# A two-layer image block on one core: layer 0's input normalisation moved from GpSimd to ScalarE, its loads and moments moved, and layer 1's first pass with the order of every engine written out

## The chip, the core and the metric

The kernel runs on one core of a Trainium2 chip. The core has a matrix engine (PE; its weight loads are shown as PEld), VectorE (DVE), ScalarE (ACT), GpSimd (POOL) and SyncE (SP), which here issues all DMA transfers. Each engine works through its own queue in order and waits on semaphores for the others. The metric is the time of one execution on the device in microseconds (us). Before the change it is 9212.45 us, the median of 3 runs (9209.08 to 9218.67).

## The reference

The input `x` has 4 images of 64 channels and 256 × 256 pixels, in f32. Two layers each add a branch to `x`, and each branch begins with a group norm over 32 groups of 2 channels (`_gn`):

```python
x = x + L0(gn(x));  x = x + L1(gn(x))

# L0: 64 -> 3*170 channels; a gate, a 3x3 depthwise branch and a spectral branch on 8x8 patches
gate, x_sp, x_fr = split(einsum('oi,bihw->bohw', w_in, x), 3)
sp = depthwise_conv3x3(x_sp, w_dw)
fr = irfft2(rfft2(patches8x8(x_fr)) * fft_weight)
out = einsum('oi,bihw->bohw', w_out, gelu(gate) * (sp + fr))

# L1: two state-space blocks, along rows (d = 0) and along columns (d = 1), then a 1x1 fusion
fx = layer_norm(x) * g + b                    # over the 64 channels of each pixel
h  = 2 * Re(C @ [scan forwards, scan backwards](B @ fx)) + D * fx
x  = gelu(h) + fx;  fx2 = layer_norm(x) * g2 + b2
y  = fx2 @ enc.T @ dec.T + fx2                # both directions, concatenated, then fusion_w
```

## The kernel before

**Layer 0.** An image is worked in 32 strips of 8 rows (`NS0`), 128 strips in all, in one software pipeline: while strip `cur` is in work, some steps of the next strip (`ahead(...)`) and of the strip before (`behind(...)`) are put between its own. The 128 partitions hold 64 channels twice, for even and odd rows or for two halves of a strip.

`load(b, s, nm, rs)` issues the DMA loads of one strip: `pr` (the patches, two transfers of 64 partitions), `at` (5 rows for each half, with the neighbours, two transfers) and `er` (4 rows for each half, two transfers). In the same call it normalises them with `normalise` (L156), a TENSOR_SCALAR on GpSimd that adds the negated mean and multiplies by the inverse deviation: `pn` from `pr` in two instructions, `at` in place, and `en` from `er`. `load` is called at the top of a strip's body, for the next strip. `at` has 3 buffers, `er` 3, `pr`, `pn` and `en` 2.

From `pn`, PE makes the spectral inputs (`spec1`, copied to SBUF as `hs` by ACT at L708; `spec2`, multiplied by the spectral weights into `hw` by VectorE). From `at`, VectorE makes sums and differences of neighbouring columns (`outer_in`, `middle_in`), which PE multiplies by the depthwise weights (`products`; ACT copies one half as `m3`, L769; VectorE joins the halves in `middle`). The last 42 hidden channels take another way: `inputs_b` makes them on PE, ACT copies them to `xat` (L743, and the row that two strips share at L734), and nine taps (`tap_b`) sum them up: tap 0 on ACT (L842), taps 1 to 8 on VectorE (L625). `gate_a` and `gate_b` make the gates on PE, with the Gelu on ACT (L804, L835). `fuse_*`, `project`, `residual` and `finish` end a strip, take its statistics for layer 1 and store it to `x1d`.

The moments of the next image are gathered meanwhile: `stat_load` brings one part of 32 a strip, `count` takes two BATCH_NORM_STATS instructions on it, and in the body of the last strip but one the last part is counted and `norm_of` makes mean and inverse deviation (an aggregate on VectorE, two small matmuls with VectorE work between, a power on GpSimd). The first strip of the next image needs them to be normalised.

**What sets the order.** The program is a list of instructions; a scheduler places each engine's instructions, by their dependencies, an estimate of their times and their place in the list. Calls through `mm` (PE) and through `vec` (VectorE, class `InOrder`) are kept in the order of the list by `tc.keep_in_program_order`. ACT, GpSimd and SP are left to the scheduler; in layer 1's first pass VectorE is as well.

**Layer 1.** For each image there are three stages: `pass_a` (first pass), `scan`, `pass_b` (second pass). `pass_a` works in 16 strips of 16 rows (`NS1`), in a pipeline in which strip `n` is centred while strip `n - 1` gets its deviation, strip `n - 2` is normalised and strip `n - 3` summarised. Its steps:

- `centre(g, i)`, for four parts: PE takes the channel mean off (`pc`), ACT writes `xc` and its square `sq` (L1059, L1060).
- `sums`, `rstd_of`, `widen`: PE sums the squares (`pv`), ACT copies the sums, PE transposes them, VectorE adds the epsilon (`ve`, L1076), GpSimd takes the power -1/2 (`rs`, L1077), and VectorE spreads it over 64 channels (`rw`, L1083, one buffer).
- `affine(g, i)`, for four parts: PE transposes `rw` (`pr`), VectorE multiplies (`z`, L1091), ACT applies gain and bias twice, for the two directions (`fv` L1095, `fh` L1099).
- `mirrored`: stores `fv` and `fh` to `fxd` and makes sums and differences of mirrored halves (`sd`, L1111): two instructions on VectorE for the columns, two on GpSimd for the rows.
- `summary_columns` and `summary_rows`: PE multiplies these by the state matrices (`pt`, `ps`), ACT copies one half (`m`, L1125, L1144), and VectorE places sum and difference in the state arrays (L1127, L1128; L1148, L1149).

Of the kernel before, what the change touches and what calls it, by code (L numbers as in the profile page):

```python
# [16 lines left out]
C = 64  # L17
HID = 170
S = 256
# [89 lines left out]
def tile_kernel(ctx: ExitStack, tc: tile.TileContext, x, cst, w0, winp, wdwp, w1, out):  # L109
# [45 lines left out]
    def normalise(o, i, nm, rs):  # L155
        nc.gpsimd.tensor_scalar(o, i, nm, rs, ALU.add, ALU.mult)  # L156
# [27 lines left out]
    with ExitStack() as l0:  # L184
# [83 lines left out]
        with ExitStack() as l1w:  # L268
# [347 lines left out]
            norm = group_norm(moments(new(gpool, [P, 2], "mv"), stats1), pw, "pw", "1")  # L616
# [4 lines left out]
        class InOrder:  # L621


            def __getattr__(self, name):
                return lambda *args, **kw: tc.keep_in_program_order(getattr(nc.vector, name)(*args, **kw))  # L625

        vec = InOrder()
# [11 lines left out]
        out_stats, last_at, n_loads = {}, {}, [0]  # L639

        def load(b, s, nm, rs):
            if s == 0:
                out_stats[b] = new(wk, [P, 2 * NS0, 6], "stats2")
            r0 = s * R0
            er = new(ld, [P, 4, S], "er", 3)
            pr = new(ld, [P, R0, 128], "pr")
            at, xat = ats[n_loads[0] % 3], xats[n_loads[0] % 2]
            n_loads[0] += 1
            for k in range(2):
                h = slice(k * C, (k + 1) * C)  # L650
                nc.sync.dma_start(out=pr[h], in_=x[b, :, r0 : r0 + R0, k * 128 : (k + 1) * 128])
# [7 lines left out]
            pn = new(wk, [P, 8, 2, R0, 8], "pn")  # L659
            for w in range(2):  # L660
                normalise(pn[:, :, w], pr[:, :, w * 64 : (w + 1) * 64].rearrange("p r (t c) -> p t r c", c=8), nm, rs)
            lo, hi = (1 if s == 0 else 0), (4 if s == NS0 - 1 else 5)
            normalise(at[:, lo:hi, 1 : S + 1], at[:, lo:hi, 1 : S + 1], nm, rs)
            if s == 0:
                nc.gpsimd.memset(at[0:C, 0, 1 : S + 1], 0.0)
                normalise(at[C:P, 0, 1 : S + 1], at[C:P, 0, 1 : S + 1], nm[C:P], rs[C:P])
            if s == NS0 - 1:
                nc.gpsimd.memset(at[C:P, 4, 1 : S + 1], 0.0)
                normalise(at[0:C, 4, 1 : S + 1], at[0:C, 4, 1 : S + 1], nm[0:C], rs[0:C])

            v14, v23 = new(wk, [P, 5, S], "v14"), new(wk, [P, 5, 2, 128], "v23")
            en = new(wk, [P, 4, S], "en")
            normalise(en, er, nm, rs)
            xen = new(wk, [P, 4, S + 2], "xen")
            return {
                "er": er, "at": at, "pn": pn, "en": en, "b": b, "s": s, "stats2": out_stats[b], "xat": xat, "xen": xen,
                "v14": v14.rearrange("p r (c k) -> p r k c", k=2), "v23": v23, "v": v14,
                "hs": new(wk, [P, 2, 4, 2, HID], "hs", 1), "hw": hws[s % 2],
            }
# [15 lines left out]
        def spec1(t, i):  # L695

            ps = new(pp, [P, 2, 512], "two")
            tiles = TILES[i]
            n = len(tiles)
            for k, tile_ in enumerate(tiles):  # L700
                for h in range(2):
                    p = slice(h * C, (h + 1) * C)
                    mm(
                        ps[:, h, k * HID : (k + 1) * HID], lhsT=t["pn"][p, tile_].rearrange("p w r c -> p (w r c)"),
                        rhs=wt0("wfr")[p, h * HID : (h + 1) * HID], start=True, stop=True,
                    )
            hs = t["hs"][:, tiles[0] % 2, tiles[0] // 2 : tiles[0] // 2 + 3] if n == 3 else t["hs"][:, :, 3]
            nc.scalar.copy(hs.rearrange("p k h c -> p h k c"), ps[:, :, : n * HID].rearrange("p h (k c) -> p h k c", k=n))  # L708
# [17 lines left out]
        def inputs_b(t):  # L726

            b, s = t["b"], t["s"]
            if s == 0:
                ps = new(pp, [P, 2, 512], "two").rearrange("p q (r c) -> p (q r) c", c=S)  # L730
                mm(ps[:, 0], lhsT=xb, rhs=t["at"][:, 0, 1 : S + 1], start=True, stop=True)
                nc.scalar.copy(t["xat"][:, 0, 1 : S + 1], ps[:, 0])
            else:
                nc.scalar.copy(t["xat"][:, 0], last_at[b][:, 4])  # L734
# [8 lines left out]
            nc.scalar.copy(t["xat"][:, 1:5, 1 : S + 1], ps)  # L743
            last_at[b] = t["xat"]
# [3 lines left out]
        def products(t, half, name, third):  # L748
# [20 lines left out]
            nc.scalar.copy(t["m3"], ps.rearrange("p e k m c -> p e k (m c)")[:, :, 1])  # L769
# [27 lines left out]
        def gate_a(t, half):  # L797
# [6 lines left out]
            nc.scalar.activation(t["ge"], pg.rearrange("p e x -> p (e x)"), AF.Gelu)  # L804
# [21 lines left out]
        def gate_b(t):  # L826
# [8 lines left out]
            nc.scalar.activation(t["geb"], ps, AF.Gelu)  # L835

        def tap_b(t, k):
            dy, dx = k // 3, k % 3
            src = (t["xat"][:, 0:4], t["xen"], t["xat"][:, 1:5])[dy]
            if k == 0:  # L840
                t["acc"] = new(wk, [P, 4, S], "acc")
                nc.scalar.activation(t["acc"], src[:, :, dx : dx + S], AF.Copy, scale=taps[:, 0:1])  # L842
# [43 lines left out]
        cur = load(0, 0, *norm)  # L886
# [11 lines left out]
        nxt_stats = None  # L898
        for b in range(nb):
            for s in range(NS0):  # L900
                if b + 1 < nb:
                    if s == 0:
                        nxt_stats = new(wk, [P, 2 * NS0, 6], "stats1")
                        counted = {0: stat_load(ld, b + 1, 0)}
                    if s + 1 < NS0:
                        counted[s + 1] = stat_load(ld, b + 1, s + 1)
                if s + 1 < NS0:
                    nxt = load(b, s + 1, *norm)
                elif b + 1 < nb:
                    nxt = load(b + 1, 0, *norm)  # L910
                else:
                    nxt = None

                def count(s, k):
                    if b + 1 < nb and s + 1 < NS0:
                        vec.bn_stats(nxt_stats[:, 2 * s + k, :], counted[s][:, k * 512 : (k + 1) * 512])
# [19 lines left out]
                count(s, 0)  # L936
                count(s, 1)
                behind(fuse_a, 1)
                products(cur, 0, "m23", False)
                middle(cur)  # L940
# [8 lines left out]
                behind(residual)  # L949
                behind(finish, 0)  # L950
# [23 lines left out]
                if s == NS0 - 2 and b + 1 < nb:  # L974
                    for k in range(2):
                        vec.bn_stats(nxt_stats[:, 2 * s + 2 + k, :], counted[s + 1][:, k * 512 : (k + 1) * 512])
                    norm = norm_of(nxt_stats)
# [58 lines left out]
    def pass_a(b, x0):  # L1036
        with ExitStack() as es:
# [17 lines left out]
            def centre(g, i):  # L1055
# [3 lines left out]
                nc.scalar.activation(xc, ps, AF.Identity, bias=off)  # L1059
                nc.scalar.activation(sq, ps, AF.Square, bias=off)  # L1060
                g["xc", i], g["sq", i] = xc, sq

            def sums(g):
# [5 lines left out]
                nc.scalar.copy(g["sums"], ps)  # L1069

            def rstd_of(g):
# [4 lines left out]
                nc.vector.tensor_scalar(ve, ps.rearrange("p (n c) -> p n c", c=32)[:, :, 0:2], LN_EPS, None, ALU.add)  # L1076
                nc.gpsimd.tensor_tensor(r, ve.rearrange("p n c -> p (n c)"), mhalf, ALU.pow)  # L1077
                g["rs"] = r

            def widen(g):  # L1080

                g["r"] = new(wk, [P, 32, C], "rw", 1)
                nc.vector.tensor_copy(g["r"], g.pop("rs").unsqueeze(2).to_broadcast([P, 32, C]))  # L1083

            def affine(g, i):
# [5 lines left out]
                nc.vector.tensor_tensor(  # L1091
# [3 lines left out]
                nc.scalar.activation(  # L1095
# [3 lines left out]
                nc.scalar.activation(  # L1099
# [4 lines left out]
            def mirrored(s, g):  # L1104

                for d, n, e in ((1, 4, nc.vector), (0, 8, nc.gpsimd)):
                    f = g.pop("fv" if d else "fh")
                    nc.sync.dma_start(out=fxd[b][s, d], in_=f.rearrange("p a b -> p (a b)"))
                    for k, op in enumerate((ALU.add, ALU.subtract)):
                        t = g["sd", d, k] = new(wk, [P, n, 1024 // n], f"sd{d}", 3)  # L1110
                        e.tensor_tensor(t, f[:, :n], f[:, : n - 1 : -1], op)  # L1111

            def summary_columns(g, s, k):
# [8 lines left out]
                if k == 0:  # L1122
                    return
                m = new(wk, [P, 256], "m")
                nc.scalar.copy(m, ps[:, 256:])  # L1125
                pv, mv = (t.rearrange("p (q g) -> p q g", q=16) for t in (ps[:, :256], m))
                nc.vector.tensor_tensor(along_columns(sf[1], 1, s), pv, mv, ALU.add)  # L1127
                nc.vector.tensor_tensor(along_columns(sb[1], 0, s), pv, mv, ALU.subtract)  # L1128

            def summary_rows(g, s, k):  # L1130
# [10 lines left out]
                if k == 0:  # L1141
                    return
                m = new(wk, [P, 2, P], "m")
                nc.scalar.copy(m, ps[:, :, P : 2 * P])  # L1144
                for hi in range(2):
                    c = slice(hi * C, (hi + 1) * C)
                    pv, mv = (t[:, :, c].rearrange("p k (r g) -> p k r g", r=4) for t in (ps, m))
                    nc.vector.tensor_tensor(along_rows(sf[0], 1, s, hi), pv, mv, ALU.add)  # L1148
                    nc.vector.tensor_tensor(along_rows(sb[0], 0, s, hi), pv, mv, ALU.subtract)  # L1149
# [9 lines left out]
            for n in range(NS1 + 3):  # L1159
                if n + 1 < NS1:  # L1160
                    got[n + 1] = {"x": load_strip(b, n + 1)}
                for i in range(4):
                    at(n, centre, i)
                    if i == 1:
                        at(n - 1, rstd_of)
                    at(n - 2, affine, i)
                    at(n - 3, (summary_columns, summary_rows)[i // 2], n - 3, i % 2)
                at(n, sums)
                if 0 <= n - 2 < NS1:
                    mirrored(n - 2, got[n - 2])  # L1170
                at(n - 1, widen)

# [63 lines left out]
    def pass_b(b):  # L1236

        with ExitStack() as es:
# [35 lines left out]

            class InOrder:


                def __getattr__(self, name):
# [282 lines left out]
```

## Time and profile before

The profiled execution took 9225.5 us, with a span of 9223.7 us from the first to the last instruction. Its stages, by the first and last instructions of each:

| stage | from (us) | to (us) | length (us) |
|---|---|---|---|
| preparation | 0 | 182 | 182 |
| layer 0, tap 0 of the first strip to tap 0 of the last | 182.0 | 4356.8 | 4174.8 |
| first pass of image 0, first centring to last placement | 4404.9 | 4680.5 | 275.7 |
| first pass of images 1, 2, 3 | 5601.2, 6805.7, 8011.1 | 5884.4, 7089.3, 8294.3 | 283.2, 283.6, 283.2 |
| second pass of image 0, first to last output | 4826.9 | 5601.1 | 774.2 |

A page shows one execution. An engine's busy share says how much of the span it worked, not whether its work was on the path. In a line of the time order the columns are: start, length, engine, source line, operation, output and inputs, shape, and how many instructions the line joins; a bracket at the end gives the engine's idle time just before it and what ended that. In a line of stages the columns are named in its first row; behind the engines come the granted PE clock, the share of the DMA engines and GB/s. A helper's line stands for all its calls: L197 is `mm` of layer 0, L625 is `vec` of layer 0, L1049 is `mm` of the first pass, L1273 and L1279 are `mm` and `vec` of the second.

### The profile page before, as it was taken

Reading aid. Unit: us, or ns where it says so; the run is one execution under the profiler, and the core shown is the slowest. Engines: PE = TensorE matmul, PEld = TensorE weight load, DVE = VectorE, ACT = ScalarE, POOL = GpSimd, SP = SyncE. Lnnn points to the kernel's source line nnn. Section 1 sums busy time; section 2 is a strip of 40 time slices with the busy share of each in tenths; the row PEclk is TensorE's granted clock in tenths of the full one; section 3 lists DMA queues with packets and bytes.
Section 4 is the critical chain, followed back from the end, with each engine's and each line's share of the span. In section 5 each row is a group of like instructions: output and inputs, shape, how many; then the busy total and the mean of one; then the engine's idle time right before and its main releaser. Section 6 shows DMA issues by size and latency. Waiting matters only on the chain. (4 is left out here: it accounts for less than half of the span.)

```text
span 9223.7 us, 183034 instructions
## 1 busy us (share of the span) xinstructions
PE 8686.5 (94%) x78454; PEld 5732.1 (62%) x78454; DVE 7299.4 (79%) x8833; ACT 2924.4 (32%) x4698; POOL 3345.0 (36%) x1798
## 2 busy tenths in 40 slices
PE   3999999999999999999889999999999999999999
PEld 2666666666666666666546665566665666665666
DVE  7999999998999989998677676767757667667776
ACT  2222222222222222222632225422245222362222
POOL 4222122221222212221664445644447444465443
PEclk9999999999999999999999999999999999999999
DMA  7444444444444433332622335323345233461332
GB/s 170 102 104 102 101 98 104 102 101 96 102 103 102 101 83 85 85 86 66 185 98 78 88 83 151 134 69 88 84 125 173 56 88 82 104 193 59 87 80 72
DMA packets 655578, 938.42 MB, mean 102 GB/s; under 512 B 43184, under 2 KB 584880, under 8 KB 619184
## 3 DMA queue, kind: packets, MB, share of 16 engines
q1 hardware_dynamic: 654768, 926.71, 38.6%
q8 instruction: 619, 10.14, 0.5%
q14 instruction: 191, 1.56, 0.1%
HBM read 583.86 MB, written 275.05 MB: 93 GB/s over the span
## 5 line engine op out<-in xcount | busy, mean ns | idle before, releaser
L197 PE MATMUL m<-v,sw 64*128 64x256 f32 (+1 forms) x8192 | 1546.0, 393 | 1.0 <-DVE v L625 0.9
L197 PEld LDWEIGHTS m<-v,sw 64*128 64x128 f32 (+1 forms) x8192 | 1136.7, 188 | 489.5 <-issue 350.4
L1376 POOL TENSOR_TENSOR xr<-xr,fx 128x512 f32<-128x512 f32 x512 | 651.3, 1272 | 1861.0 <-ACT xr L1375 1367.2
L1273 PE MATMUL pst<-fx,wb 64*128 64x256 f32 (+1 forms) x4992 | 1015.8, 437 | 37.4 <-DVE stm L1279 18.3
L625 DVE SCALAR_TENSOR_TENSOR acc<-xat,taps,acc 128x1024 f32<-128x1024 f32 x640 | 975.2, 1524 | 14.4 <-ACT acc L842 0.7
L156 POOL TENSOR_SCALAR pn<-pr,nm,rs 128x512 f32<-128x512 f32 x256 | 412.9, 1621 | 1376.9 <-issue 968.0
L804 ACT ACTIVATE ge<-two 128x1024 f32<-128x1024 f32 x256 | 262.8, 1027 | 1794.9 <-DVE hw L625 1706.4
L156 POOL TENSOR_SCALAR at<-at,nm,rs 128x1280 f32<-128x1280 f32 (+2 forms) x136 | 199.8, 1469 | 1624.9 <-DMA at<-in_x_dram 1565.5
L1273 PEld LDWEIGHTS pst<-fx,wb 64*128 64x128 f32 (+1 forms) x4992 | 508.1, 186 | 370.9 <-issue 244.3
L1406 POOL TENSOR_TENSOR rs<-ve,mhalf 128x32 f32<-128x32 f32 x128 | 695.5, 5433 | 99.3 <-DVE ve L1279 99.3
L1279 DVE SCALAR_TENSOR_TENSOR stm<-stm,step,pst 128x512 f32<-128x512 f32 x640 | 478.5, 748 | 232.8 <-PE pst L1273 219.3
L1377 ACT ACTIVATE sq<-xr 128x512 f32<-128x512 f32 x512 | 322.7, 630 | 875.4 <-POOL xr L1376 875.4
L197 PEld LDWEIGHTS m<-ct,hw 128*64 128x64 f32 x16384 | 509.3, 138 | 118.1 <-issue 118.1
L1273 PE MATMUL px<-wb,xr 128*128 128x128 f32 x4096 | 574.7, 284 | 0.0
L1279 DVE SCALAR_TENSOR_TENSOR sto<-sto,step,pst 128x512 f32<-128x512 f32 x512 | 382.8, 748 | 242.1 <-PE pst L1273 230.8
L625 DVE TENSOR_TENSOR hw<-two,wsp 128x1020 f32<-128x1020 f32 (+1 forms) x384 | 423.6, 1103 | 175.5 <-PE two L197 161.8
L1273 PEld LDWEIGHTS px<-wb,xr 128*128 128x128 f32 x4096 | 524.5, 194 | 54.2 <-issue 41.8
L1279 DVE TENSOR_TENSOR y<-px,rs 128x512 f32<-128x512 f32 x512 | 354.0, 691 | 231.4 <-PE px L1273 222.4
L1273 PE MATMUL ph<-sto,wb 128*64 128x128 f32 (+1 forms) x5120 | 528.0, 299 | 0.0
L197 PE MATMUL m<-ct,hw 128*64 128x64 f32 x16384 | 527.1, 223 | 0.0
L1273 PE MATMUL ph<-stm,wb 128*64 128x128 f32 (+1 forms) x5120 | 525.0, 299 | 0.0
L1273 PEld LDWEIGHTS ph<-stm,wb 128*64 128x64 f32 (+1 forms) x5120 | 408.9, 147 | 144.6 <-issue 128.1
(317 smaller groups left out, 16571.6 us busy)
## 6 DMA issues: line engine op xcount, KB each, us to landing
strip<-x1d SPq DMA_DIRECT2D x512, 256.0 KB, 7.3
fx<-fxd SPq DMA_DIRECT2D x128, 1024.0 KB, 6.9
at<-in_x_dram SPq DMA_DIRECT2D x248, 320.0 KB, 5.4
xen<-xat SPq DMA_DIRECT2D x256, 258.0 KB, 5.0
sx<-in_x_dram SPq DMA_DIRECT2D x256, 256.0 KB, 4.0
pr<-in_x_dram SPq DMA_DIRECT2D x256, 256.0 KB, 4.1
er<-in_x_dram SPq DMA_DIRECT2D x256, 256.0 KB, 4.5
x1d<-x SPq DMA_DIRECT2D x256, 256.0 KB, 3.6
```

Source lines behind the costliest of these rows:

```text
L156: nc.gpsimd.tensor_scalar(o, i, nm, rs, ALU.add, ALU.mult)
L197: tc.keep_in_program_order(nc.tensor.matmul(*args, **kw))
L625: return lambda *args, **kw: tc.keep_in_program_order(getattr(nc.vector, name)(*args, **kw))
L804: nc.scalar.activation(t["ge"], pg.rearrange("p e x -> p (e x)"), AF.Gelu)
L1273: tc.keep_in_program_order(nc.tensor.matmul(*args, **kw))
L1279: return lambda *args, **kw: tc.keep_in_program_order(getattr(nc.vector, name)(*args, **kw))
L1376: nc.gpsimd.tensor_tensor(xr, xr, fx, ALU.add)
L1377: nc.scalar.activation(sq, xr, AF.Square)
L1406: nc.gpsimd.tensor_tensor(r, ve.rearrange("p n c -> p (n c)"), mhalf, ALU.pow)
```

## The change

In layer 0, ACT normalises in place of GpSimd, by an activation with a scale and a shift (`scale_of` makes the shift from mean and deviation). `load` is taken apart: `load_patches` and `load_rows` issue the loads, and `normal_rows(n + 1)` and `normal_patches(n + 2)` normalise, both between `products(cur, 0, "m23", False)` and `middle(cur)`. The loads are issued behind `residual`: rows two strips ahead, patches three. The copy of the shared row of `xat` moves from `inputs_b` to `normal_rows`. The parts for the moments are loaded and counted two a strip in strips 0 and 1 and one a strip up to strip 29, at whose end `norm_of` now stands. ACT is kept in the order of the list (`act`).

In the first pass, ACT, VectorE and GpSimd are kept in the order of the list (`act`, `vec`, `gps`), steps are split (`scaled_in` from `affine`, `store` from `mirrored`, `place_columns` and `place_rows` from the summaries), and the body's order is written out. A strip is summarised four steps behind its centring, where it was three; the first half of the column summary stays at three.

```diff
-    def normalise(o, i, nm, rs):
-        nc.gpsimd.tensor_scalar(o, i, nm, rs, ALU.add, ALU.mult)
+    vec, act, gps = InOrder(nc.vector), InOrder(nc.scalar), InOrder(nc.gpsimd)
...
+        def normalise(o, i, b, p=slice(0, P)):
+            rs, shift = norm[b]
+            act.activation(o, i, AF.Identity, bias=shift[p], scale=rs[p])
+
+        def normal_patches(n):
...
+            pn = t["pn"] = new(wk, [P, 8, 2, R0, 8], "pn")
             for w in range(2):
-                normalise(pn[:, :, w], pr[:, :, w * 64 : (w + 1) * 64].rearrange("p r (t c) -> p t r c", c=8), nm, rs)
+                normalise(pn[:, :, w], pr[:, :, w * 64 : (w + 1) * 64].rearrange("p r (t c) -> p t r c", c=8), t["b"])
+
+        def normal_rows(n):
...
-            normalise(at[:, lo:hi, 1 : S + 1], at[:, lo:hi, 1 : S + 1], nm, rs)
+            normalise(at[:, lo:hi, 1 : S + 1], at[:, lo:hi, 1 : S + 1], b)
...
+            en = t["en"] = new(wk, [P, 4, S], "en")
+            normalise(en, t["er"], b)
...
+            if s > 0:
+                act.copy(t["xat"][:, 0], strips[n - 1]["xat"][:, 4])
...
+        parts = [(2 * s, 2 * s + 1) if s < 2 else (s + 2,) if s + 2 < NS0 else () for s in range(NS0)]
...
                 tap_b(cur, 2)
-                count(s, 0)
-                count(s, 1)
+                count()
                 behind(fuse_a, 1)
                 products(cur, 0, "m23", False)
+                if nxt is not None:
+                    normal_rows(n + 1)
+                normal_patches(n + 2)
                 middle(cur)
...
                 behind(residual)
+                load_rows(n + 2)
+                load_patches(n + 3)
+                if s + 1 < NS0:
+                    load_parts(b, s + 1)
+                elif b + 1 < nb:
+                    load_parts(b + 1, 0)
                 behind(finish, 0)
...
-                if s == NS0 - 2 and b + 1 < nb:
-                    for k in range(2):
-                        vec.bn_stats(nxt_stats[:, 2 * s + 2 + k, :], counted[s + 1][:, k * 512 : (k + 1) * 512])
-                    norm = norm_of(nxt_stats)
+                if s == NS0 - 3 and b + 1 < nb:
+                    norm[b + 1] = scale_of(*norm_of(nxt_stats), b + 1)
...
-            for n in range(NS1 + 3):
+            for n in range(NS1 + 4):
                 if n + 1 < NS1:
                     got[n + 1] = {"x": load_strip(b, n + 1)}
-                for i in range(4):
-                    at(n, centre, i)
-                    if i == 1:
-                        at(n - 1, rstd_of)
-                    at(n - 2, affine, i)
-                    at(n - 3, (summary_columns, summary_rows)[i // 2], n - 3, i % 2)
-                at(n, sums)
-                if 0 <= n - 2 < NS1:
-                    mirrored(n - 2, got[n - 2])
-                at(n - 1, widen)
+                at(n, centre, 0)
+                at(n - 2, affine, 0)
+                at(n - 1, sums)
+                at(n - 2, scaled_in, 0)
+                at(n - 3, mirrored, 1)
+                at(n - 4, summary_columns, n - 4, 1)
+                at(n, centre, 1)
+                at(n - 2, affine, 1)
+                at(n - 1, rstd_of)
+                at(n - 2, scaled_in, 1)
+                at(n - 4, place_columns, n - 4)
+                at(n - 4, summary_rows, n - 4, 0)
+                at(n, centre, 2)
+                at(n - 2, affine, 2)
+                at(n - 2, scaled_in, 2)
+                at(n - 4, summary_rows, n - 4, 1)
+                at(n, centre, 3)
+                at(n - 2, affine, 3)
+                at(n - 4, place_rows, n - 4)
+                at(n - 2, scaled_in, 3)
+                at(n - 2, store, n - 2)
+                at(n - 3, summary_columns, n - 3, 0)
+                at(n - 1, widen)
+                at(n - 3, mirrored, 0)
```

## The prediction

> **What bounds the kernel now.** I read the page first, then tables of stages, then single strips in order of time. The page:
>
> ```profile
> span 9223.7 us, 183034 instructions
> PE 8686.5 (94%) x78454; PEld 5732.1 (62%) x78454; DVE 7299.4 (79%) x8833; ACT 2924.4 (32%) x4698; POOL 3345.0 (36%) x1798
> ```
>
> PE is nearly always busy, so a gain has to be time in which PE waits for another engine. The change touches two stages: layer 0 (182 to about 4390 us) and the four first passes of layer 1 (about 276 us for the first, 283 for each other). Scan and second pass keep their instruction order on PE and VectorE.
>
> Layer 0. The tap-0 activation (L842) marks the strips: 182.04 us for the first, 4356.84 for the last, so 4174.8 us for 127 steps. Most take 32.2 to 33.3 us; the last two steps inside each image take 31.1; the step from one image to the next takes 44.2, 45.3 and 44.7. The table of stages for an ordinary strip, a fast one, and a step between images:
>
> ```profile
> core 0: us, PE busy (x) PEld busy (x) DVE busy (x) ACT busy (x) POOL busy (x), PEclk, DMA share, GB/s
> 506.77:539.27 32.50, 31.46 (x356) 20.58 (x354) 30.36 (x31) 9.36 (x11) 6.52 (x4) 1.00 0.43 102
> 1126.69:1157.81 31.12, 31.12 (x356) 20.64 (x354) 29.02 (x31) 9.36 (x12) 1.20 (x1) 1.00 0.35 88
> 1188.94:1233.18 44.24, 36.20 (x362) 23.92 (x364) 32.05 (x36) 9.32 (x11) 16.20 (x12) 0.88 0.44 99
> ```
>
> The fast strip has 1.20 us of POOL in place of 6.52, and PE has no gap at all: 31.12 is PE's floor for this order. What POOL does to VectorE is in the time lines of the ordinary strip, POOL first:
>
> ```profile
> 513.88 1.42 POOL L156 TENSOR_SCALAR at<-at,nm,rs 128x1280 f32<-128x1280 f32 x1 [13.88 <-DMA at<-in_x_dram]
> 515.27 2.17 POOL L156 TENSOR_SCALAR en<-er,nm,rs 128x1024 f32<-128x1024 f32 x1
> ...
> 514.79 3.71 DVE L625 SCALAR_TENSOR_TENSOR acc<-xat,taps,acc 128x1024 f32<-128x1024 f32 x2
> ```
>
> and VectorE's same two taps, and ACT's second gate, in the fast strip:
>
> ```profile
> 1134.70 2.59 DVE L625 SCALAR_TENSOR_TENSOR acc<-xat,taps,acc 128x1024 f32<-128x1024 f32 x2
> ...
> 1146.09 1.02 ACT L804 ACTIVATE ge<-two 128x1024 f32<-128x1024 f32 x1 [12.62 <-DVE hw L625]
> ```
>
> The taps lose 1.12 us to the normalisations, two residual adds behind them another 0.29 (1.66 against 1.36), and PE then waits for VectorE's `hw`: the strips differ by 1.38 us. ACT stands idle for 12.62 us in mid-strip.
>
> First pass of layer 1. In steady state a strip takes 16.03 us (start to start of L1083). PE, VectorE and POOL in one such strip, each in its order of time:
>
> ```profile
> 4536.48 0.60 PE L1053 MATMUL pr<-ct,rw 128*128 128x128 f32 x4
> 4537.01 2.06 PE L1049 MATMUL ps<-sd,wa 64*128 64x128 f32 x32
> 4538.99 1.13 PE L1049 MATMUL pc<-strip,cenr 128*128 128x512 f32 x2
> 4539.96 0.60 PE L1053 MATMUL pr<-ct,rw 128*128 128x128 f32 x4
> ...
> 4528.74 4.53 DVE L1111 TENSOR_TENSOR sd<-fv 128x1024 f32<-128x1024 f32 x2 [1.49 <-ACT fv L1095]
> ...
> 4529.55 5.96 POOL L1111 TENSOR_TENSOR sd<-fh 128x1024 f32<-128x1024 f32 x2 [4.70 <-PE pv L1049]
> 4535.46 5.43 POOL L1077 TENSOR_TENSOR rs<-ve,mhalf 128x32 f32<-128x32 f32 x1
> ```
>
> Differences of PE's starts give what a group costs: `pr` 0.44 to 0.53, `ps` 1.98, `pc` 0.86 to 0.97, `pt` 1.73, `pv` of squares 1.72. A strip's sum: pc 3.64, pr 1.94, pt 3.46, ps 3.97, pv 1.72 + 0.43: 15.2 us. So at most 0.85 us a strip can be won there by order alone. The `sd` pairs show the two engines taking turns: VectorE's lone one lasts 1.22 and its second, beside POOL's, 3.38; POOL's last 2.64 and 3.36, of which 2.2 is its own work and the rest the wait for VectorE's to end.
>
> **The change, part by part.**
>
> 1. Normalisation from POOL to ACT, behind the `m3` copy. Per strip ACT gains at (1280 columns), en (1024), two pn (512) and keeps the halo copy (0.39), which moves there. By rows: the tap-0 activation, 1024 columns, 1.15; fv with scale and bias tiles, 512 columns, 0.81; hence about 1.4 + 1.15 + 1.6 + 0.4 = 4.6 us. The Trainium skill speaks against the engine ("ScalarE: Activation LUTs", rules for kernel authors: add and mul belong on VectorE); its price on the same page (280 ns, 93 for a second pointer operand, 0.833 a column) makes 1.44 + 1.23 + 0.80 + 0.80 + 0.39 = 4.7. Either lies in the 12.62 us hole: m3 ends 6.8 us into a strip, so the block ends at 11.5 and the gate wants ACT at 19.4. Cost 0, with 7.9 us of cover; beyond it every us costs a strip a us. Behind the block on ACT stand that gate, hs and m3, and PE behind those. `middle_in` of the next strip needs `at` at 13.2 and has it at 8.2. Gain: strips fall to 31.12.
>
> 2. Loads. Their number is nearly the same: four row and two patch issues a strip, at about 0.6 us each on SP, beside sx, x1d and xen. In the built order `at` is asked for two strips ahead and `er` behind the residual, at 14.5 us of the strip before: 25 us before ACT wants it, against 4.0 to 5.4 us to landing. The half `at` load ahead of xen waits for readers that are done before xen's own source: no new wait. Cost 0; the cover is 20 us.
>
> 3. Moments two strips ahead. A step between images costs 13.1 us over the floor (44.24 − 31.12), of which the rows name
>
> ```profile
> 1192.77 0.35 PE L139 MATMUL two<-mv,ct 128*128 128x1 f32 x2 [4.19 <-DVE mv L174]
> ...
> 1199.40 0.94 PE L197 MATMUL two<-w0t,pn 64*128 64x170 f32 x4 [2.93 <-POOL pn L156]
> ```
>
> Afterwards strips 0 and 1 count twice as much (two BATCH_NORM_STATS more, 1.36 less 0.19 of slack before `y`: 1.17 each), strip 29 has the aggregate in mid-strip (1.89 less slack: 1.6) and the chain mean, variance behind hw(2), about 1.4 of PE waiting; strip 31 keeps the extra top row (1.5). Sum 6.9 an image step.
>
> Layer 0: first step 29.0 as now, 126 × 31.12 = 3921.1, 3 × 6.9 = 20.7: 3970.8 against 4174.8, −204. At the start ACT's copies of hs stand behind the second strip's patches: +1.5 (0 to 4). **−202.5.**
>
> 4. First pass in fixed order. The row and column mirrors part: VectorE's pair follows z0, POOL's comes last, behind its power (`rs`). Measure from the first `pr` of a strip. The second `pr` starts at 0.47 + 1.78 + 1.73 + 0.86 = 4.84 (pr, sums, pt, pc). From there two chains run. POOL: z1 starts 0.70 later (transposes to z in the ramp: 5629.69 to 5630.39), ve 0.88 after, 0.18 long, power 0.1 later, 5.43 long, first mirror 2.2: the second mirror begins at 4.84 + 9.46 = 14.3 and holds to 16.5. VectorE: pv, ps, pc, pr, ps, pc as above, 7.39, then z3 at +0.70, 0.88 long, four placements at 0.2: `widen` is asked for at 4.84 + 9.77 = 14.6. So widen comes 0.3 us too late to slip between the mirrors. If the two exclude each other it runs after 16.5, ends at 17.55, and the next strip's first `pr`, which waits for it, at 17.6.
>
> Do they? The trace has only the other case: at 4654.18 POOL's mirror was issued with 0.26 of widen left and took 2.46, not 2.2. The Trainium skill ("GPSIMD Engine Reference", key points) says the SBUF interfaces are shared, with contention for VectorE instructions in a 2-port mode or with two SBUF inputs; widen moves 2048 columns in 1.21 us, where a two-input add moves 1024 in 1.22. This rule speaks against the new order: by it a strip takes 17.6 us; by the rows of widen alone (1186 to 1229 ns, 64 times) it takes 14.6 + 1.21 + 0.06 = 15.9. I take the rule, since `sd` behaves by it.
>
> Per image, first to last widen is 231.6 us now. With the collision: 13.1 (the second strip waits for its power, where 9.0 sufficed), 15.4 (PE has no summaries yet, so widen is asked for during the first mirror), 12 × 17.6, 15.4 (no centring left, the same): 255.1. The drain, 27.3 us now: widen 1.3; z3 of the last strip at 10.2 behind VectorE's and POOL's turns; fv and fh to 11.6; mirrors by turns to 17.8; last row summary to 19.9; copy and placements to 21.3: 22.6. Together +18.8; four images **+75** (±16 for the drain). Bounds for the stage: PE's floor 15.2 in all 14 strips, −60; the collision, +75.
>
> Sum: −202.5 + 75 = −127.5. The profiled execution took 9225.5 us (span 9223.7), so 9098; the runs' median 9212.45 lies 13 lower, so **9085**.
>
> **The rivals.**
> - *B, no collision* (widen slips past, or isn't held): 13.1 + 13.4 + 12 × 15.9 + 13.9 = 231, drain −4.7: −21 in four images. −223.5: **8989**. For it: 0.3 us is little beside chains of 14 us. Against: anything that delays VectorE there falls deeper into the mirror, which is 2.2 long.
> - *C, layer 0 wins half*: ACT's stream, or landings, stretch VectorE as POOL did; 0.4 to 0.7 us a strip stay, some 70 us: **9155**. Against: in the first pass ACT runs beside z and widen, whose times spread by 6%.
> - *D, slower*: ACT in fixed order stands before a late load (L156's operations, now ahead of the second gate). It decides from 8.9 us late in every strip: 7.9 of cover, then 1.0 × 127 strips eat the 127.5 us. `er` would have to land about 34 us after its issue rather than 4.5; at 12 us late the time is 9212 + 127 × 3.1: **9606**. Against: DMA share 0.43.
>
> **How the numbers follow.** A 0.55, B 0.30, C 0.11, D 0.03, no net effect 0.01. A alone spreads 9055 to 9115 (drain ±16, start and image steps ±10), B 8970 to 9010. The range 8970 to 9120 leaves out C, D and the edges. 0.2% (18 us) is about what a measurement of this kernel tells from no change; faster by more: A, B, C = 0.96, same 0.01, slower 0.03.
>
> **What would show it.** Right: strips of 31.1 us with PE without gap, POOL idle in layer 0, ACT's block ending before the gate; image steps at 6 to 8 us over; in the first pass widen lasting about 3 us and strips of 17.6. B: widen 1.2 us, strips 15.4 to 15.9. Wrong: `ge` waiting for ACT behind a DMA, taps still 1.6 to 2.1 us, or PE waiting in the first pass for something other than `rw`.

## The result

The changed kernel takes 9124.6 us (median of 4 runs, 9120.6 to 9136.41); the kernel before, on the same chip, 9215.56 us (9209.08 to 9219.34). The ratio is 0.9904, with a 95% interval of 0.9887 to 0.9921: 1.0% faster, 91 us. The prediction was 9085, with a range up to 9120: the sign is right, the gain is 36 us smaller than forecast, and the time lies 4.6 us above the range.

The page of the changed kernel:

```profile
span 9126.5 us, 182410 instructions
PE 8613.1 (94%) x78454; PEld 5705.4 (63%) x78454; DVE 7105.8 (78%) x8837; ACT 3460.7 (38%) x5218; POOL 2406.8 (26%) x1278
```

POOL has lost 938 us and ACT has gained 536, as the move says. How the 97 us between the two spans come about, by stage, in us:

| stage | before | after | difference | forecast |
|---|---|---|---|---|
| layer 0, first tap-0 activation to last | 4174.8 | 3964.1 | −210.7 | −204.0 |
| start of layer 0 | 182.0 | 182.1 | 0 | +1.5 |
| four first passes, first `pc` to last `sb` | 1125.7 | 1246.7 | +121.0 | +75 |
| the rest (transitions, scan, second pass) | | | −7.5 | 0 |

**Layer 0.** The table of stages for an ordinary strip and the first two strips of a step between images (columns as in the prediction):

```profile
core 0: us, PE busy (x) PEld busy (x) DVE busy (x) ACT busy (x) POOL busy (x), PEclk, DMA share, GB/s
507.44:538.44 31.00, 31.00 (x358) 20.42 (x356) 28.94 (x31) 13.27 (x15) 0.00 (x0) 1.00 0.44 107
1052.50:1085.30 32.80, 32.80 (x376) 22.06 (x374) 30.75 (x32) 14.55 (x17) 0.31 (x1) 1.00 0.46 114
1085.30:1118.30 33.00, 30.43 (x340) 19.36 (x338) 29.79 (x36) 12.26 (x14) 0.57 (x1) 1.00 0.41 100
```

A strip takes 31.0 us; PE has no gap in it and POOL does nothing. ACT's lines of that strip in order of time, from the middle copy to the next gate:

```profile
529.89 0.59 ACT L162 COPY m<-m 128x512 f32<-128x512 f32 x1 [0.87 <-PE m L205]
530.37 1.46 ACT L162 ACTIVATE at<-at,shift,rs 128x1280 f32<-128x1280 f32 x1
531.73 1.23 ACT L162 ACTIVATE en<-er,shift,rs 128x1024 f32<-128x1024 f32 x1
532.86 0.40 ACT L162 COPY xat<-xat 128x258 f32<-128x258 f32 x1
533.16 1.53 ACT L162 ACTIVATE pn<-pr,shift,rs 128x512 f32<-128x512 f32 x2
543.02 1.03 ACT L162 ACTIVATE ge<-two 128x1024 f32<-128x1024 f32 x1 [8.33 <-PE two L205]
```

The block costs 4.3 us (4.6 to 4.7 forecast) and ends 8.33 us ahead of the gate. The two taps of VectorE that took 3.71 us beside POOL take 2.60:

```profile
531.72 2.60 DVE L301 SCALAR_TENSOR_TENSOR acc<-xat,taps,acc 128x1024 f32<-128x1024 f32 x2
```

At a step between images PE's wait for the moments, 4.19 us before, is now two short ones:

```profile
1115.49 0.38 PE L139 MATMUL two<-mv,ct 128*128 128x1 f32 x2 [0.38 <-ACT xat L162]
1116.70 0.35 PE L148 MATMUL two<-var,ct 128*128 128x1 f32 x2 [0.83 <-DVE var L145]
```

A step between images costs 6.7 to 7.5 us above five ordinary strips (32.81 + 32.99 + 32.38 + 32.13 + 32.32 − 5 × 31.03 = 7.5; forecast 6.9).

**First pass.** One strip, 17.3 us long, in order of time; POOL first, then VectorE, then PE:

```profile
4317.71 5.44 POOL L162 TENSOR_TENSOR rs<-ve,mhalf 128x32 f32<-128x32 f32 x1 [7.25 <-DVE ve L301]
4323.12 4.68 POOL L162 TENSOR_TENSOR sd<-fh 128x1024 f32<-128x1024 f32 x2
...
4325.44 0.28 DVE L301 TENSOR_TENSOR sb<-ps,m 128x128 f32<-128x128 f32 x1
4325.64 3.24 DVE L301 COPY rw<-rs 128x2048 f32<-128x2048 f32 x1
...
4329.03 0.63 PE L1100 MATMUL pr<-ct,rw 128*128 128x128 f32 x4 [2.51 <-DVE rw L301]
```

POOL's two mirrors run from 4323.12 to 4327.80, the second from about 4325.45. VectorE reaches `rw` at 4325.64, 0.2 us after it began, and the copy takes 3.24 us where it took 1.21. PE stands for 2.51 us. This is the collision of the prediction, with its place and nearly its size. Over all four images the view of `rw` reads, before and then after:

```profile
L1083 DVE COPY rw<-rs x64: 1186/1210/1229, 4421.6 to 8266.7; 128x2048 f32<-128x2048 f32 x64
...
  DVE rw L1083: 21.6, 12
```

```profile
L301 DVE COPY rw<-rs x64: 1226/3234/3364, 4210.2 to 8165.6; 128x2048 f32<-128x2048 f32 x64
...
  DVE rw L301: 199.5, 68
```

(shortest, median and longest copy in ns; then how long PE and its weight loads, in us and times, stood idle until `rw`.) What the prediction doesn't have is a second kind of strip: 16 of the steps from one `rw` to the next take 18.7 to 19.0 us, not 17.3.

### The profile page after: what moved, and what is told of

The parts are those of the page before. It is cut to its first block, busy times and chain, and to the rows that moved or that the text cites. A ratio compares the mean times of both kernels' runs of the same rounds, so it can differ in the third digit from the quotient of the medians.

```text
span 9126.5 us, 182410 instructions
## 1 busy us (share of the span) xinstructions
PE 8613.1 (94%) x78454; PEld 5705.4 (63%) x78454; DVE 7105.8 (78%) x8837; ACT 3460.7 (38%) x5218; POOL 2406.8 (26%) x1278
## 5 line engine op out<-in xcount | busy, mean ns | idle before, releaser
L301 DVE SCALAR_TENSOR_TENSOR acc<-xat,taps,acc 128x1024 f32<-128x1024 f32 x640 | 820.6, 1282 | 15.3 <-ACT acc L162 1.6
L301 DVE TENSOR_TENSOR z<-xc,pr 128x512 f32<-128x512 f32 x256 | 265.1, 1037 | 386.2 <-PE pr L1100 378.8
```

## The experiments

Theory: the two halves of the change are independent; layer 0 gains 211 us because POOL no longer delays VectorE; the first pass loses because `rw` is asked for just after POOL's second mirror starts and has to wait until it ends. Open were: whether the engines exclude each other or merely share; what makes the strips of 19.0 us; why the last strips of a pass take 29 us and not 22.6.

### The two halves alone

Layer 0 as changed, with `pass_a` of the kernel before:

> Layer 0 as changed, the first pass as before. Theory (the two halves of the change add up): the layer-0 gain of 210.7 us read from the trace stays whole and the first pass falls back to 275 to 284 us an image: 9215 - 211 = 9004 us (8990 to 9015). Rival (the first pass is slow because of what the new layer 0 leaves behind, its pools or its clock): the first passes stay above 300 us and the time above 9080.

Measured: 9006.5 us, ratio 0.977 (0.9757 to 0.9784). Layer 0 takes 3963.8 us, the first passes 275.7 to 282.7.

The reverse, `pass_a` of the changed kernel in the kernel before:

> Layer 0 as before, the first pass in its new order. Theory: + 121 us, so 9336 us (9315 to 9350), with first passes of 300 to 318 us, the column sums' copy rw lasting about 3.2 us, and strips of 17.3 and 19.0. Rival (part of the 121 us comes with the new layer 0): under 9280.

Measured: 9324.4 us, ratio 1.0116 (1.0102 to 1.013), + 108; `rw` has a median of 3.23 us. The profiled execution is the shortest of the four (9309.45). Its first passes take 300.1, 310.5, 307.4 and 309.8 us, 1227.9 together: 102 more than before, and 19 less than in the changed kernel. It has 13 of the 19.0 us strips instead of 16, and 15.6 of the 19 us are time in which PE was busy with the same instructions (1005.5 against 1021.1). The halves add up within what was measured: −210 and + 108 make −102; for both it was −91, by its interval −73 to −104.

### Which engine normalises

```
-            act.activation(o, i, AF.Identity, bias=shift[p], scale=rs[p])
+            gps.tensor_scalar(o, i, rs[p], shift[p], ALU.mult, ALU.add)
```

> The changed kernel with the normalisations of layer 0 on POOL again, in the new order and with the new loads. Theory (the engine is what counts: POOL's two-operand work makes VectorE's taps wait): strips of 32.2 to 33.3 us again, about 1.4 us for each of 127 strips: + 180 us, 9305 us (9270 to 9330); taps beside the normalisations at 1.8 us. Rival (the gain is from order and earlier loads): strips stay near 31.1, below 9160 us.

Measured: 9270.9 us, ratio 1.0057 (1.0044 to 1.0071), 146 us above the changed kernel; strips of 32.3 us. In its time lines (POOL, then VectorE):

```profile
508.50 2.49 POOL L162 TENSOR_SCALAR at<-at,rs,shift 128x1280 f32<-128x1280 f32 x1
...
508.46 3.60 DVE L301 SCALAR_TENSOR_TENSOR acc<-xat,taps,acc 128x1024 f32<-128x1024 f32 x2
```

The engine is worth 146 of layer 0's 211 us: the same work on POOL again stretches the pair of taps from 2.60 to 3.60. The remaining 65 us are what the new order keeps with POOL at work: its image steps cost 4 to 5 us over five of its ordinary strips, where the kernel before has 9 to 10, and its ordinary strips are 32.3 where the kernel before has 32.2 to 33.3. Expected were 180 us for the engine; the new order does more by itself than was thought, 65 us and not 31.

### Is ACT's block really free?

`en` and both patch tiles are normalised five times each, with the same result:

```
+            for _ in range(5):
-            normalise(en, t["er"], b)
+                normalise(en, t["er"], b)
...
+                for _ in range(5):
-                normalise(pn[:, :, w], ...)
+                    normalise(pn[:, :, w], ...)
```

> The changed kernel with the normalisations of en and of the two patch tiles on ACT done five times each instead of once. By the trace each round costs 1.13 + 1.44 = 2.57 us, so ACT's block in mid-strip grows by 10.3 us; it ends 8.3 us before the second gate is due. Theory (the block is hidden as far as that cover reaches and costs one for one beyond it): 10.3 - 8.3 = 2.0 us a strip, 127 strips: + 254 us, 9380 us (9300 to 9450). If the cover were less, or VectorE were disturbed by ACT: up to 10.3 us a strip, 10400 us; if ACT's order had more slack behind the gate: 9125.

Measured: 9203.7 us, ratio 0.9989 (0.9983 to 0.9996): + 79 over the changed kernel, a third of what was expected. ACT in a strip that begins (tap 0) at 521.50:

```profile
529.53 6.34 ACT L162 ACTIVATE en<-er,shift,rs 128x1024 f32<-128x1024 f32 x5
535.77 0.39 ACT L162 COPY xat<-xat 128x258 f32<-128x258 f32 x1
536.07 8.30 ACT L162 ACTIVATE pn<-pr,shift,rs 128x512 f32<-128x512 f32 x10
544.28 1.00 ACT L162 ACTIVATE ge<-two 128x1024 f32<-128x1024 f32 x1
```

The block ends 22.9 us into the strip and not 11.0; it has grown by 11.9 us, more than the 10.3 worked out. The gate starts at 22.8, in the changed kernel at 19.3: 3.5 us late. But the strips answer in two ways: in the first three images every second one takes 32.4 us and the others 31.0; in the last image, where VectorE counts no moments, all take 31.0. That is 60 us in layer 0 (4024.5 against 3964.1); 21 us more lie ahead of its first tap (202.7 against 182.1). So the cover reaches further than the gate: PE and VectorE have slack behind it. That the counting uses up this slack fits the last image, but was not tried. "Beyond it every us costs a strip a us" is too strong.

### Exclusion or sharing

The last `z` of each strip is computed twice (same result), so that `rw` is asked for 0.9 us later:

```
+                for _ in range(2 if i == 3 else 1):
-                vec.tensor_tensor(z..., xc..., ps..., ALU.mult)
+                    vec.tensor_tensor(z..., xc..., ps..., ALU.mult)
```

> The changed kernel with the last z of each strip computed twice on VectorE (0.88 us more, from PSUM), so that widen is asked for 0.9 us later, deeper in POOL's second mirror. Exclusion (the copy starts when the mirror ends, whenever it was asked for): rw is shorter by 0.9 us, 2.3 us, strips stay at 17.3, the time within 10 us of 9125. Shared bandwidth (the copy runs slowly beside the mirror): its end moves by half to all of the delay, strips 17.7 to 18.2, + 25 to + 45 us.

Measured: 9120.3 us, ratio 0.9899 (0.9884 to 0.9914), the same as the changed kernel; steady strips 17.3. POOL, then VectorE:

```profile
4303.48 4.68 POOL L162 TENSOR_TENSOR sd<-fh 128x1024 f32<-128x1024 f32 x2
...
4304.34 2.11 DVE L301 TENSOR_TENSOR z<-xc,pr 128x512 f32<-128x512 f32 x2 [2.43 <-PE pr L1100]
...
4307.08 2.17 DVE L301 COPY rw<-rs 128x2048 f32<-128x2048 f32 x1
```

0.9 us more work ahead, and `rw` is 1.07 shorter: it ends at 4309.25, 1.1 us after the mirrors' end at 4308.16, just as in the strip of the changed kernel shown above (4328.88 and 4327.80). This is a lock, not shared bandwidth. The Trainium skill has it so ("SBUF — State Buffer", section "SBUF: two separate sides"): the port pair that VectorE and GpSimd share is held for a whole instruction by whichever came first, and the other blocks. The `z` pair beside it, which reads one operand from PSUM, is not held (1.05 each).

### Out of the way: three places

`widen` ahead of the four row placements:

```
+                at(n - 1, widen)
                 at(n - 4, place_rows, n - 4)
...
-                at(n - 1, widen)
                 at(n - 3, mirrored, 0)
```

> The changed kernel with widen moved ahead of the four row placements on VectorE, so that it is asked for 0.8 us earlier, while POOL's first mirror still runs. Theory (the two engines exclude each other for whole instructions, and the copy comes 0.2 to 0.3 us too late): rw slips between the two mirrors and waits at most 0.7 us, strips take 15.2 to 15.6 us, no half-clock window is left in them: 4 x (13 x 1.9 + 8) = 130 us less than the changed kernel, 8995 us (8975 to 9020). Rival (the engines share the bandwidth, and rw is slow wherever it runs beside a mirror): rw still takes about 3 us, the strip gains the 0.8 us alone: 9083 us.

Measured: 8984.9 us, ratio 0.9749 (0.9735 to 0.9762). POOL, VectorE, PE:

```profile
4310.44 5.69 POOL L162 TENSOR_TENSOR sd<-fh 128x1024 f32<-128x1024 f32 x2
...
4312.18 1.71 DVE L301 COPY rw<-rs 128x2048 f32<-128x2048 f32 x1
...
4314.03 0.63 PE L1100 MATMUL pr<-ct,rw 128*128 128x128 f32 x4 [0.20 <-DVE rw L301]
```

Asked for during the first mirror, `rw` gets in between the two (1.71 us), and now POOL's pair is the one that waits: 5.69 us in place of 4.68. Strips take 15.0 us, PE's own work. 140 us for moving one line.

POOL's first mirror ahead of its power, `widen` left last:

```
                 at(n, centre, 0)
+                at(n - 3, mirrored, 0, (0,))
...
                 at(n - 1, widen)
-                at(n - 3, mirrored, 0)
+                at(n - 3, mirrored, 0, (1,))
```

> The changed kernel with POOL's first mirror moved to the start of the strip, ahead of its power, the second left where it is; widen stays last on VectorE. Theory (what counts is only whether a mirror runs when rw is asked for): the power ends 2.4 us before the end of POOL's second mirror as it now stands, so that mirror is over at 14.3 to 14.7 us after the first pr, rw is asked for at 14.6 and waits 0.1 us at most: strips of 15.6 to 15.9, no half-clock window: 4 x (13 x 1.5 + 8) = 110 us under the changed kernel, 9015 us (8990 to 9040). Rival (the place of widen in VectorE's order is what counts, not POOL's mirror): strips of 17.3, 9125 us.

Measured: 8992.4 us, ratio 0.9755 (0.974 to 0.9769); `rw` 1.22 us, strips 15.3. VectorE's order is untouched here, so the collision alone was what cost.

Both mirrors first, with four buffers, and `widen` ahead of the placements:

```
                 at(n, centre, 0)
+                at(n - 3, mirrored, 0)
...
+                at(n - 1, widen)
                 at(n - 4, place_rows, n - 4)
...
-                at(n - 1, widen)
-                at(n - 3, mirrored, 0)
```

> The changed kernel with both of POOL's mirrors at the start of the strip (four buffers for them), ahead of its power, and widen ahead of the row placements: no mirror can be running when rw is asked for. Theory: rw takes 1.2 us in the steady strips, not 3.2, nor the 1.7 of the version that only moves widen; but PE's own work of 15.0 us is the floor that this version already reached: 8985 us (8970 to 9000). Rival (the mirrors, now beside the column mirrors on VectorE, delay z1 and so the power): strips of 16 to 17 us, 9040 to 9090.

Measured: 8988.3 us, ratio 0.9749 (0.9735 to 0.9764); `rw` 1.23, strips 14.8 to 14.9.

### What makes 19.0 us of 17.3

In the 19.0 us strips PE's second `pt` group takes 3.3 us to the start of the next group, in place of 1.83, with nothing waited for:

```profile
4382.70 3.48 PE L1096 MATMUL pt<-sd,wa 128*128 128x256 f32 x8
4386.02 1.02 PE L1096 MATMUL pc<-strip,cenr 128*128 128x512 f32 x2
```

Windows of 3.41 us of the changed kernel, in pairs; the column after POOL's is the granted clock:

```profile
core 0: us, PE busy (x) PEld busy (x) DVE busy (x) ACT busy (x) POOL busy (x), PEclk, DMA share, GB/s
4273.09:4276.50 3.41, 1.44 (x5) 0.56 (x3) 3.41 (x5) 2.75 (x4) 2.72 (x2) 1.00 1.05 313
4276.50:4279.91 3.41, 2.87 (x18) 1.76 (x19) 2.60 (x4) 1.15 (x2) 0.00 (x0) 1.00 1.01 404
4378.91:4382.32 3.41, 1.33 (x12) 0.58 (x12) 2.60 (x2) 0.89 (x2) 0.85 (x1) 1.00 1.04 402
4382.32:4385.74 3.42, 3.42 (x11) 2.48 (x8) 2.55 (x3) 2.00 (x3) 0.00 (x0) 0.50 1.01 323
```

PE busy for 1.44 of 3.41 us: full clock goes on. Busy for 1.33: the next window has half. In each first pass the clock records lie on a grid of 3.413 us. With PE's records laid on it, 33 stretches of half clock begin in the four passes or just ahead of them, each after a window in which PE was busy for 43% or less; and of the 275 windows at full clock with another such window behind them, the least busy has 41%. The border lies thereabouts. Each of the 16 slow steps holds 3.4 us of half clock. Of the steps of 17.3 to 17.5 us only the last one of three images holds any; the last one of the other image has none and takes 14.6. A wait of 2.5 us falls inside one window, or across two, by chance; only the first costs a half-clock window, 1.7 us. To test it, PE gets more to do in the gap:

```
+                if i == 0:
+                    mm(ps, lhsT=cen, rhs=g["xc", 0], start=True, stop=True)
                 turn_blocks(ps, lambda k: g["r"]...)
```

> The changed kernel with one matrix product more per strip on PE (512 columns, some 0.9 us, its result overwritten), placed before the first pr, in the 2.5 us in which PE waits for rw. Theory (the strips of 19.0 us are those in which PE stood idle for 60% or more of a 3.41 us window, after which the clock is halved for the next window; the wait alone makes strips of 17.3): with 1.6 us of idle time the windows of half clock go from the steady strips and all are 17.3, 8 to 16 strips x 1.65 us less in spite of more work: 9105 us (9095 to 9118). Rival (the strips of 19.0 come from something that PE waits for): no change, or + 0.9 us where PE is behind: 9125 to 9140.

Measured: 9094.5 us, ratio 0.9863 (0.9846 to 0.9879): 30 us faster with more work. `rw` still takes 3.24 us. PE:

```profile
4321.22 1.02 PE L1096 MATMUL pr<-xc,cenr 128*128 128x512 f32 x2
4323.81 0.66 PE L1100 MATMUL pr<-ct,rw 128*128 128x128 f32 x4 [1.57 <-DVE rw L301]
```

All later strips are 17.2 to 17.3; above 18.5 there is only one per image, at its start, where the wait is longer. It is the clock.

### The drain

From the last `rw` to the last `sb` a pass takes 29.1, 29.2, 30.2 and 30.4 us; forecast 22.6, before 27.3. On the version with both mirrors early (drain 30.1), in the iteration of the last affine step:

```
+                if n == NS1 + 1:
+                    at(n - 3, mirrored, 0)
+                    for i in range(4):
+                        at(n - 2, affine, i)
+                        at(n - 2, scaled_in, i)
...
+                    continue
```

> On the version with both mirrors early and widen ahead of the row placements: in the drain of a first pass the four z of the last strip come ahead of the strip before's column mirrors and placements on VectorE, and its transposes ahead of the summaries on PE. Theory (the drain of 29 to 30 us is long because the last strip's z stand behind other strips' work, and mirrors, summaries and placements wait in one chain behind them): z3 ends 5 us after rw instead of 9 to 10, the drain falls by 5 to 9 us an image: 8988 - 28 = 8960 us (8950 to 8970). Rival (the drain is bound by POOL's six mirrors in turns with VectorE's, wherever z stands): no change, 8985 to 8992.

Measured: 8984.7 us, ratio 0.9752 (0.9737 to 0.9766), no gain; drain 30.2. The last `z` is done 5.5 us after `rw`'s end, but the end of the drain stays. Neither is it POOL, as the rival had it: its last mirror is over 13 us before the end. PE's lines of this drain:

```profile
4438.32 2.02 PE L1100 MATMUL pr<-ct,rw 128*128 128x128 f32 x8 [0.26 <-DVE z L301]
4440.13 2.68 PE L1096 MATMUL pt<-sd,wa 128*128 128x256 f32 x8
4442.74 3.84 PE L1096 MATMUL ps<-sd,wa 64*128 64x128 f32 x64
4446.51 3.72 PE L1096 MATMUL pt<-sd,wa 128*128 128x256 f32 x16
4450.16 3.84 PE L1096 MATMUL ps<-sd,wa 64*128 64x128 f32 x64
4453.93 3.72 PE L1096 MATMUL pt<-sd,wa 128*128 128x256 f32 x16
4457.58 3.84 PE L1096 MATMUL ps<-sd,wa 64*128 64x128 f32 x64
```

PE runs without a gap through the summaries of three strips, 3 × 7.4 us less half a `pt`. They are left over because the new order takes a strip's summaries partly one iteration later than before (`n - 4` and `n - 3`, where it was `n - 3`). So one strip fewer should be left over: all summaries and placements in the iteration `n - 3`, on the early mirrors:

```
-            for n in range(NS1 + 4):
+            for n in range(NS1 + 3):
...
-                at(n - 4, summary_columns, n - 4, 1)
-                at(n - 4, place_columns, n - 4)
-                at(n - 4, summary_rows, n - 4, 0)
+                at(n - 3, summary_rows, n - 3, 0)
...
-                at(n - 4, summary_rows, n - 4, 1)
+                at(n - 3, summary_rows, n - 3, 1)
...
-                at(n - 4, place_rows, n - 4)
+                at(n - 3, place_rows, n - 3)
...
                 at(n - 3, summary_columns, n - 3, 0)
+                at(n - 3, summary_columns, n - 3, 1)
+                at(n - 3, place_columns, n - 3)
```

> Both mirrors of POOL early, and the summaries and placements one strip sooner (of the strip three behind, all within one pass of the loop, where the changed kernel takes one half a pass later). Theory (the drain is PE's own queue: in the version before this one PE ran without a gap through three strips' summaries, 3 x 7.4 us, whatever VectorE and POOL did): one strip's summaries fewer after the last rw, the drain 30 to 22 or 23 us, 7.4 us an image: 8985 - 30 = 8955 us (8945 to 8970), if the steady strip stays at 14.9 to 15.1. Rival (z1 waits for the mirrors by turns, and the power and rw with it; or column placements late): strips of 15.5 to 16 and the gain is eaten: 8985 to 9010.

Measured: 8972.9 us, ratio 0.9727 (0.9713 to 0.974), just above the range; strips 14.8. In this order the columns are placed last. VectorE's last `rw` and last `sb` of the pass, and PE's last summaries:

```profile
4426.59 3.35 DVE L301 COPY rw<-rs 128x2048 f32<-128x2048 f32 x1 [3.72 <-POOL rs L162]
...
4454.32 0.57 DVE L301 TENSOR_TENSOR sb<-pt,m 128x256 f32<-128x256 f32 x1
...
4444.40 2.06 PE L1096 MATMUL ps<-sd,wa 64*128 64x128 f32 x32 [1.75 <-POOL sd L162]
4447.69 2.06 PE L1096 MATMUL ps<-sd,wa 64*128 64x128 f32 x32 [1.23 <-POOL sd L162]
4449.67 3.72 PE L1096 MATMUL pt<-sd,wa 128*128 128x256 f32 x16
```

The drain is 28.3, 26.9, 26.9 and 27.2 us, 2.8 less in the mean than with the early mirrors and not the 7.4 of the theory. Behind the last `rw` PE has a strip's `ps` and half a `pt` fewer, 5.7 us, but it now waits 3.0 us for POOL's last mirrors. So PE's queue did bound the drain, and with that queue shortened POOL's mirrors are the next bound. The four passes together are 17 us shorter than with the early mirrors (1087.5 against 1104.6); the ratio moves by 0.0022, 20 us, and the two intervals still touch. The last `rw` of a pass is still held in both versions: a mirror of POOL starts 0.07 us ahead of it. This version has the lowest time: 2.7% under the kernel before, 1.7% under the changed one.

## Why the prediction was right, and where it was wrong

1. *Normalisation to ACT, gain to PE's floor*: right. Strips 31.0 against 31.12, block 4.3 us against 4.6, no gap on PE, and the engine shown as the larger part of the cause. The price beyond the cover was wrong, by the run with longer work on ACT: 3.5 us of lateness cost 0.7 us a strip in the first three images and nothing in the last.
2. *Loads at no cost*: right as far as the trace shows; the gate waits for PE and not for a load. It wasn't tried alone.
3. *Moments two strips ahead*: 6.7 to 7.5 us a step against 6.9. The first tap is not later than before; the first two steps take 30.1 and 32.1 us, where 29.0 and 31.1 were forecast, and what of this is the start's 1.5 was not separated. Layer 0 in all: −210.7 against −202.5.
4. *First pass*: the mechanism was right, and the choice of the exclusion over the undisturbed rows, which decided between the forecast and rival B, was right by the runs with `rw` moved and delayed. `rw` was forecast to start 0.3 us too late and was 0.2 too late; strips 17.6 against 17.3. (The forecast's 17.55 for its end is short of its own figures: 16.5 and 1.21 make 17.7. Measured, the copy ends 1.08 us after the mirror.) The step that failed is the size of this term, + 75, which was also taken for the stage's upper bound. It failed in three parts of its own sum:
   - the drain, "z3 of the last strip at 10.2 … mirrors by turns to 17.8; last row summary to 19.9 … 22.6". It follows VectorE and POOL, and leaves out PE's own queue. That could be read from the prediction's rows: `pt` 3.46 and `ps` 3.97 a strip, 2.5 and 3 of them, and `pr` 1.94 make 22.5 us of PE from the first `pr` of the last strip to the last summary, where the forecast has 19.9. Measured in image 0: 24.9, with 1.9 us of waits for VectorE in it. The last `rw` is held too (2.73 us for 1.3), so that the first `pr` comes 1.6 us later. Of the 6.6 us in this drain 2.6 are PE's queue, 1.9 the waits, 1.6 `rw` and 0.5 the rest; images 2 and 3 have some of the half clock besides. Four drains: 118.9 against 90.4 us, + 28.5.
   - "12 × 17.6" has no term for the clock. Sixteen strips of 18.7 to 19.0 are 1.4 to 1.7 us longer each, some 26 us, and the last steps with half clock in them take 17.3 to 17.5 against 15.4; the shorter steady strip and ramp give more than half of it back. First to last `rw` of the four images: 1033.2 us against 1020.4, + 12.8.
   - what lies ahead of the first `rw`: 94.6 us against 89.3, + 5.2; the cause stays open.

   Together 46.5 us: 75 becomes 121, to within half a us.

The sum −127.5 thus becomes −210.7 + 121.0 = −90; the −7.5 of the remaining stages was not traced to a part of the change, and the medians show −91.

Rival B (8989) was what happened as soon as the collision was taken away: 8985 to 8992. That the totals agree so well is in part luck: B has strips of 15.9 and a drain of 22.6, and with `widen` moved they were 15.0 and 29.8. Rivals C and D did not occur: the taps take 1.28 us in the mean of all 1024, and ACT's gate waits for PE.

## What to carry to other kernels

Where GpSimd and VectorE both work from SBUF, fix the order of both together: a mirror that started 0.2 us ahead of `rw` held it to its own end, and one line moved was worth 140 us here. A wait that is added to PE should be priced with the clock: in this kernel it costs its length, and where it leaves PE idle for more than about 58% of a 3.4 us window, another 1.7 us; dummy work in the gap was worth 30 us. At the end of a pipelined loop, count PE's leftover queue as well as the other engines' chains: with 5.7 us of summaries taken out of it the drain here fell by 2.8, for POOL then held PE up.

## What was not expected of the hardware

The clock was halved by waits of 2.5 us. The Trainium skill ("TensorE: Matmul & The Clock Gate", section "HAM oscillation — how this bites in real kernels") puts the limit at idle gaps above some 3.4 us; in this kernel a window of 3.413 us that is 39% busy is enough, with 2.1 us of the gap inside it (the third row of the windows above). The same wait costs nothing or 1.7 us depending on where it falls on that grid, so two versions with the same order can differ in the first passes, as the changed kernel and its first pass in the old one did: 1246.7 against 1227.9 us, of which 15.6 are PE's busy time.

Whether the lock holds a copy with a single SBUF input was the open point of the prediction. It does: `rw`, 1.21 us alone, is held for as long as 2.1 us. And it works in both directions, as POOL's pair, stretched from 4.68 to 5.69 us, shows.
